# Layer 0's softmax weights from a second score product with keys on rows, and layer 1's transposes in another pair of PSUM banks

## The chip, the core and the metric

The kernel runs on one NeuronCore of one Trainium2 chip. TensorE (PE) multiplies matrices into PSUM, ScalarE (ACT) evaluates exponentials and copies, VectorE (DVE) reduces and multiplies, GpSimd (POOL) works on SBUF only, SyncE (SP) starts DMAs. Each of these engines takes its instructions in the order in which the kernel writes them. The metric is the device time of one execution in microseconds, as a median over runs.

## What is computed

Two cross-attention layers follow each other, for 8 batch elements, 256 queries of 320 channels and 20 heads of 16 channels. Cut to the core:

```python
# layer 0: 77 text keys and 179 image keys, a softmax of its own over each
out_text = attend(q, k,    v)        # attend: softmax(q k^T / 4) v
out_ip   = attend(q, k_ip, v_ip)
x1 = (out_text + out_ip) @ Wo.T + bo + x
# layer 1: 252 text keys; 4 image keys, whose scores get a term from the text weights
probs_t  = softmax(q k_t^T / 4);  text_out = probs_t @ v_t
qsem     = l2norm(probs_t @ text_ehs)
fused    = q k_ip^T / 4 + 0.5 * qsem . l2norm(ip_ehs)
ip_out   = (softmax(fused) * mask) @ v_ip
out = (text_out + ip_out) @ W_out + b_out + x1
```

All data is 32-bit floating point.

## The kernel before, in words

**Units.** Four heads of one batch element and one layer make a unit, so each layer has 5 units per element and 40 in all. The units of an element are counted g = 0 to 4. The main loop has 46 steps n (L1227): step n treats unit n of layer 0 and unit n - 6 of layer 1 (SHIFT, L47), and it finishes the values of the layer 1 unit that was begun one step earlier. Steps 0 to 39 run `both_layers` (L1148), the last six `layer_1` (L1194).

**The order is written by hand.** `tc.manual_schedule` (L79) keeps PE, DVE, ACT and POOL in the order of the source. A step is a fixed row of calls with seven gaps, numbered 0 to 6, and `fillers(n, place)` (L1023) puts work that belongs to no unit into them, from a table by g and gap: projections of queries, keys and values of both layers (`l0_q`, `l0_k`, `l0_v`, `l1_q`, `l1_k`, `l1_v`), the Gram matrix of the text (`l1_gram`), the output projections (`l0_out`, `l1_out`) and layer 1's image part.

**PSUM.** Four banks `sc0` to `sc3` hold the scores of one unit, one bank for each head (2 x 256 values on 128 partitions). Two banks `mm` serve the fillers, two banks `y` the value products.

**A unit of layer 0.** `scores` (L355) multiplies in 8 products, with queries on rows. `l0_max` (L500) takes 8 maxima on DVE. `l0_exp` (L510) runs 16 exponentials on ACT from PSUM into SBUF, one for each head, half of the queries and key group, and each sums its row. `l0_transposed` (L523) turns each head in four 128x128 transposes on PE, back into the head's own score bank, and copies the bank to SBUF (three heads on DVE, one on ACT, L407). `l0_values` (L526) multiplies by the values, with text and image kept apart in 2 x 16 rows. In the next step `l0_attn` (L545) transposes that product back to queries on rows (L553), divides by the sums on DVE (L558) and adds text and image on POOL. `l0_attn_T` (L575) transposes the whole element again for the output projection.

**A unit of layer 1.** `l1_begin` (L692) multiplies the scores into the same banks `sc0` to `sc3`. Then come 4 maxima on DVE (L716), 8 exponentials on ACT (L731), 16 transposes back into the score banks (L400) and 4 copies. In the next step `l1_values` (L742) makes, for each head and half, a product y (L755, L758) in a `y` bank and two DVE instructions that empty it (L762, L766).

**A step in old order.** Scores 0, maxima 0, exponentials 0 of heads 0 and 1, gap 0, the other exponentials; then on PE the 16 transposes of layer 0 mixed with the products y of heads 0 and 1, gaps 1 and 2, y of head 2, gap 3; scores 1, maxima 1, exponentials 1, gap 4, half of y of head 3, transposes of heads 0 and 1 of layer 1, gap 5, the other half of y, the other transposes, gap 6, values 0. Masked queries (`masked_q`, L348) come from POOL ahead of each score product.

Of the kernel before, what the change touches and what calls it, by code (L numbers as in the profile page):

```python
# [8 lines left out]
F32 = mybir.dt.float32  # L9
# [24 lines left out]
TXT0 = 77  # L34
TXT1 = 252
# [11 lines left out]
SHIFT = NQ + 1  # L47


@with_exitstack  # L50
def kernel(
# [97 lines left out]
    wo, wo1 = new_c("wo"), new_c("wo1")  # L149
# [23 lines left out]
    zeros = work.tile([P, S], F32, tag="qz", name="zeros", bufs=2)  # L173
# [5 lines left out]
    one = small.tile([P, 1], F32, tag="one", name="one", bufs=1)  # L179
    nc.vector.memset(one, 0.0)  # L180
    nc.scalar.activation(one, one, AF.Exp)
# [25 lines left out]
    for j in (5, 7):  # L207
        nc.vector.tensor_tensor(quad_m[:, 2:3], quad_m[:, 2:3], head_m[:, j : j + 1], ALU.add)

    tok_m = const.tile([P, 2], F32, tag="tok_m", name="tok_m")  # L210
    nc.gpsimd.memset(tok_m, 1.0)
    nc.gpsimd.affine_select(
        out=tok_m[:, 0:1], in_=tok_m[:, 0:1], compare_op=ALU.is_ge, fill=0.0,
        base=TXT0 - 1, pattern=[[0, 1]], channel_multiplier=-1,
    )
    nc.gpsimd.affine_select(
        out=tok_m[:, 1:2], in_=tok_m[:, 1:2], compare_op=ALU.is_ge, fill=0.0,
        base=-TXT0, pattern=[[0, 1]], channel_multiplier=1,
    )
# [29 lines left out]
    def ip_norm(_):  # L249
        nc.scalar.activation(ip["rn"], ip["rn"], AF.Sqrt)  # L250
        table(AF.Exp)
# [96 lines left out]
    def masked_q(qT, u, name):  # L348

        m, _, i = QUADS[u]  # L350
        qz = work.tile([P, S], F32, tag="qz", name=f"{name}_qz", bufs=2)
        nc.gpsimd.tensor_scalar_mul(qz, qT[:, m, :], quad_m[:, i : i + 1])  # L352
        return qz

    def scores(qz, kT, u, name):  # L355


        sc = [ps_sc.tile([P, NH, T], F32, tag=f"sc{j}", name=f"{name}_{j}") for j in range(4)]
# [12 lines left out]
    def unit(layer, b, g, sc, home):  # L371


        name = f"{layer}_{b}_{g}"
        nmx = (P, 2, NH, 2) if layer == 0 else (P, 2, NH)

        def pairs(pool, shape, tag, bufs):
            return [
                pool.tile(list(shape), F32, tag=tag, name=f"{tag}_{name}_{x}", bufs=bufs)
                for x in range(2)  # L380
            ]

        return {
            "b": b,
            "g": g,
            "sc": sc,
            "nmx": pairs(small, nmx, f"nmx{layer}", 4),
            "e": pairs(work, (P, 2, NH, T), f"e{home}", 2 + home),
            "et": pairs(work, (P, 2, 2, NH, P), f"et{home}", 2),
        }  # L390

    def transposed_probs(u, j, tn, t0, copy=None):
# [3 lines left out]
        ps = u["sc"][j][:tn].rearrange("p n t -> p (n t)")  # L396
# [16 lines left out]
    k0 = const.tile([P, NC, T], F32, tag="k0", name="k0")  # L413


    v0 = [const.tile([P, 2, H, 2, D], F32, tag=f"v0_{i}", name=f"v0_{i}") for i in range(2)]
    for t in v0:
        nc.gpsimd.memset(t[:, 1, :, 0, :], 0.0)
# [6 lines left out]
    k1c = [const.tile([P, W_K1], F32, tag=f"k1c_{i}", name=f"k1c_{i}") for i in range(2)]  # L425
# [17 lines left out]
    def l0_k(b, m):  # L443
# [19 lines left out]
        low, high, kc = slice(0, HP), slice(HP, P), k1c[b % 2]  # L463
        if m < 2:
            nc.scalar.copy(k0[:, m, first:T], ps[:, t0 + first : t0 + T])  # L465
            if kept:
                nc.gpsimd.tensor_copy(k0[:, m, :TXT0], kt[:, m, :])
        else:

            for rows in (low, high):  # L470
                nc.scalar.copy(k0[rows, m, first:T], ps[low, t0 + first : t0 + T])
                if kept:
                    nc.scalar.copy(k0[rows, m, :TXT0], kt[low, m, :])
            for rows in (low, high):
                nc.scalar.copy(kc[rows, NIP + first : T], ps[high, t0 + first : t0 + TXT1])
                if kept:
                    nc.scalar.copy(kc[rows, NIP : NIP + TXT0], kt[high, m, :])
# [3 lines left out]
    def l0_v(b, i):  # L481

        ps = mm_tile(f"v0_{b}_{i}")
        cols = slice(0, P) if i < 2 else slice(P, T)
        project_rows(ps[:, :C], lambda k: bat[b]["encT"][:, k, cols], wv if i == 0 else wvip)
        v = ps[:, :C].rearrange("p (h d) -> p h d", d=D)
        if i < 2:
            nc.scalar.mul(v0[b % 2][:, 0, :, i, :], v, tok_m[:, i : i + 1])
        else:
            nc.scalar.copy(v0[b % 2][:, 1, :, 1, :], v)  # L490

    SPAN0 = ((0, TXT0), (TXT0, T))

    def l0_begin(b, g):
        u = unit(0, b, g, scores(qz[0], lambda j: k0[:, QUADS[g][0], :], g, f"sc0_{b}_{g}"), 0)

        u["den"] = small.tile([P, NH, 4, 2], F32, tag="den0", name=f"den0_{b}_{g}")
        return u

    def l0_max(u, x):  # L500
        for j in range(2):
            for a, (t0, t1) in enumerate(SPAN0):
                nc.vector.tensor_reduce(  # L503
                    u["nmx"][x][:, j, :, a],
                    u["sc"][2 * x + j][:, :, t0:t1],
                    AX.X,
                    ALU.max,
                    negate=True,
                )

    def l0_exp(u, x):
        for j in range(2):
            for half in range(NH):
                for a, (t0, t1) in enumerate(SPAN0):
                    nc.scalar.activation(  # L515
                        u["e"][x][:, j, half, t0:t1],
                        u["sc"][2 * x + j][:, half, t0:t1],
                        AF.Exp,
                        bias=u["nmx"][x][:, j, half, a : a + 1],
                        accum_out=u["den"][:, half, 2 * x + j, a : a + 1],  # L520
                    )

    def l0_transposed(u, j, copy=None):  # L523
        transposed_probs(u, j, P, 0, copy)

    def l0_values(u):  # L526

        name = f"{u['b']}_{u['g']}"
        o = ps_y.tile([P, S], F32, tag="y", name=f"oT_{name}")
        heads = QUADS[u["g"]][1]  # L530
        for c in range(2):
            for j, h in enumerate(heads):
                nc.tensor.matmul(  # L533
                    o[j * QP : (j + 1) * QP, :],
                    v0[u["b"] % 2][:, c, h, :, :].rearrange("p a d -> p (a d)"),
                    u["et"][j // 2][:, j % 2, c, :, :].rearrange("p n s -> p (n s)"),
                    start=(c == 0),
                    stop=(c == 1),
                )
        u["rden"] = small.tile([P, NH, 4, 2], F32, tag="rden0", name=f"rden0_{name}")  # L540
        nc.vector.reciprocal(u["rden"], u["den"])
        u["o"] = work.tile([P, S], F32, tag="oT", name=f"oT_sb_{name}", bufs=1)
        nc.scalar.copy(u["o"], o)

    def l0_attn(u):  # L545
        r = bat[u["b"]]
        m, _, i = QUADS[u["g"]]
        name = f"{u['b']}_{u['g']}"
        if u["g"] == 0:
            r["attn"] = work.tile([P, NH, C], F32, tag="attn0", name=f"attn0_{name}", bufs=1)  # L550
        ps = ps_y.tile([P, S], F32, tag="y", name=f"o0_{name}")
        for half in range(NH):
            nc.tensor.transpose(  # L553
                ps[:, half * P : (half + 1) * P], u["o"][:, half * P : (half + 1) * P], ident
            )
        rden = u["rden"]
# [18 lines left out]
    def l0_attn_T(b, half):  # L575
        r = bat[b]
        r["aT", half] = attn_T(r["attn"][:, half, :], f"p0_{b}_{half}")
# [724 lines left out]
```

## Time and profile before

| | |
|---|---|
| three runs | 879.37, 879.49, 879.64 us |
| profiled execution, first to last instruction (span) | 877.6 us |
| the median stands above that span by | 1.9 us |
| PE busy | 863.8 us, 98% of the span |
| PE's weight loads busy | 696.3 us, 79% |
| DVE busy | 612.4 us, 70% |
| ACT busy | 545.0 us, 62% |
| POOL busy | 208.5 us, 24% |
| DMA | 22.96 MB, mean 26 GB/s |

The page gives no run time of the profiled execution itself beside its span; the 1.9 us lie around the span. A group row of the profile names the source line, the engine, the operation, the tiles and shapes, the number of records, then busy time and mean nanoseconds of one, then the idle time of the engine just before such instructions and what ended it. A 32-bit product of this kernel stands as two PE records, a transpose as one: 16 records are the 8 products of one unit's scores. Means of PE records overlap, so a series is priced by the time from its start to the start of what follows.

### The profile page before, as it was taken

The numbers are of one execution on the slowest core, as the hardware profiler recorded it, in microseconds if no ns is written. First come the engines' busy times: TensorE is split into PE (matmuls) and PEld (weight loads), VectorE is DVE, ScalarE is ACT, GpSimd is POOL, SyncE is SP. The second block draws the span as 40 slices with busy tenths as digits, with TensorE's granted clock in tenths as the row PEclk, the third lists the DMA queues.
The fourth block names the chain that finished last, engine by engine and source line by source line (L and its number), as shares of the span: only waits on it lengthen the run. The fifth ranks groups of instructions, "written<-read, shape, count | busy, mean of one in ns | idle before, by whom it ended". The sixth has DMA issues, their size and how long they took to land.

```text
span 877.6 us, 18756 instructions
## 1 busy us (share of the span) xinstructions
PE 863.8 (98%) x6184; PEld 696.3 (79%) x6184; DVE 612.4 (70%) x2071; ACT 545.0 (62%) x2386; POOL 208.5 (24%) x376
## 2 busy tenths in 40 slices
PE   8999999999999999999999999999999999999998
PEld 6777678788787887888877888888888788777876
DVE  2544477767776777876778678776777778875765
ACT  4774676556664686555765468654675558754855
POOL 2212311223211222122321322212222122312111
PEclk9999999999999999999999999999999999999999
DMA  9600100001000100001001010000100100000000
GB/s 279 174 6 16 44 1 1 2 18 41 15 2 20 34 25 2 15 22 43 17 1 21 16 43 1 3 20 16 43 1 1 22 16 1 1 21 1 1 20 16
DMA packets 24624, 22.96 MB, mean 26 GB/s; under 512 B 5936, under 2 KB 24496, under 8 KB 24528
## 3 DMA queue, kind: packets, MB, share of 16 engines
q1 hardware_dynamic: 23088, 20.27, 8.8%
q10 hardware_dynamic: 1440, 1.49, 0.5%
q8 instruction: 50, 0.82, 0.4%
q14 instruction: 46, 0.38, 0.1%
HBM read 18.31 MB, written 2.62 MB: 24 GB/s over the span
## 4 chain that ended last, share of the span: by engine, by line
PE 95%; ACT 3%; DVE 1%; DMA 1%; issue 0%; SPq 0%; POOL 0%; ACTq 0%; DVEq 0%
PE y L755 17%; PE sc L400 16%; PE v L325 11%; PE sc L362 10%; PE y L758 9%; PE k L313 8%; PE q L295 7%; PE p_o L338 6%; PE oT L533 5%; PE g L624 2%; ACT e L515 1%; PE p_aT_ps L331 1%; ACT e L731 1%; PE o L553 1%; PE ipo L877 1%; DMA wk<-in_WkT_dram 1%
## 5 line engine op out<-in xcount | busy, mean ns | idle before, releaser
L515 ACT ACTIVATE e<-sc,nmx 128x77 f32<-128x77 f32 (+1 forms) x640 | 227.2, 412 | 57.4 <-DVE nmx L503 57.4
L731 ACT ACTIVATE e<-sc,nmx 128x252 f32<-128x252 f32 x320 | 147.4, 484 | 120.0 <-DVE aip L711 107.3
L755 PE MATMUL y<-gv,et 126*128 126x272 f32 x640 | 202.0, 397 | 1.3
L762 DVE CUSTOM_DVE_ANT_0 e<-y,e 128x252 f32<-128x252 f32 x320 | 133.9, 419 | 90.4 <-PE y L758 81.8
L400 PE MATMUL sc<-ident,e 128*126 128x128 f32 (+1 forms) x1280 | 182.4, 274 | 4.2 <-ACT e L731 2.8
L407 DVE COPY et<-sc 128x512 f32<-128x512 f32 (+1 forms) x229 | 154.4, 689 | 24.3 <-PE sc L400 14.5
L503 DVE TENSOR_REDUCE nmx<-sc 128x2 f32<-128x154 f32 x320 | 109.7, 416 | 87.2 <-PE sc L362 87.2
L400 PEld LDWEIGHTS sc<-ident,e 128*126 128x126 f32 (+1 forms) x1280 | 149.1, 140 | 14.2 <-ACT e L731 6.2
L515 ACT ACTIVATION_READ_ACCUMULATOR e<-sc,nmx 128x1 f32 x640 | 159.9, 250 | 0.0
L758 PEld LDWEIGHTS y<-gv,et 126*128 126x128 f32 x640 | 120.7, 189 | 25.9
L758 PE MATMUL y<-gv,et 126*128 126x146 f32 x640 | 131.4, 287 | 0.0
L716 DVE TENSOR_REDUCE nmx<-sc 128x2 f32<-128x504 f32 x160 | 106.7, 673 | 22.7 <-PE sc L362 22.7
L755 PEld LDWEIGHTS y<-gv,et 126*128 126x128 f32 x640 | 104.8, 190 | 18.2 <-issue 3.0
L568 POOL TENSOR_TENSOR attn<-o_sb 128x64 f32<-128x64 f32 x80 | 24.0, 321 | 396.3 <-DVE o_sb L558 355.2
L407 ACT COPY et<-sc 126x512 f32<-126x512 f32 (+1 forms) x91 | 52.2, 593 | 75.8 <-PE sc L400 75.7
L362 PE MATMUL sc<-k,sc_qz 32*128 32x256 f32 x1152 | 82.6, 400 | 1.0 <-ACT k L465 0.6
L352 POOL TENSOR_SCALAR sc_qz<-q,quad_m 128x256 f32<-128x256 f32 x80 | 73.2, 925 | 6.6 <-ACT q L302 6.0
L362 PEld LDWEIGHTS sc<-k,sc_qz 32*128 32x128 f32 x1152 | 52.1, 184 | 24.4 <-issue 15.3
L731 ACT ACTIVATION_READ_ACCUMULATOR e<-sc,nmx 128x1 f32 x320 | 69.7, 218 | 0.0
L325 PE MATMUL v<-wv,encT 128*126 128x324 f32 (+1 forms) x192 | 58.1, 447 | 0.0
L766 DVE COPY num<-y 128x20 f32<-128x20 f32 x320 | 55.6, 174 | 0.0
L338 PE MATMUL p_o<-wo,p_aT 128*128 128x320 f32 x180 | 53.0, 437 | 0.3 <-DVE p_aT L332 0.3
(148 smaller groups left out, 1044.7 us busy)
## 6 DMA issues: line engine op xcount, KB each, us to landing
encT<-in_encT_dram SPq DMA_DIRECT2D x7, 512.0 KB
x<-in_x_dram SPq DMA_DIRECT2D x8, 320.0 KB
out_dram<-osb SPq DMA_DIRECT2D x15, 160.0 KB
xT<-in_xT_dram SPq DMA_DIRECT2D x7, 256.0 KB
texts<-in_encT_dram SPq DMA_DIRECT2D x6, 154.0 KB
xT<-in_xT_dram SPq DMA_DIRECT2D x7, 128.0 KB
vip_rows<-vipA SPq DMA_DIRECT2D x32, 25.0 KB
wv<-in_WvT_dram SPq DMA_DIRECT2D x1, 640.0 KB
```

The source lines that it names most:

```text
L325: nc.tensor.matmul(ps, lhsT(k), w[:, k, :], start=(k == 0), stop=(k == NE - 1))
L338: nc.tensor.matmul(ps[:, :C], aT[:, m, :], w[:, m, :], start=(m == 0), stop=(m == NC - 1))
L362: nc.tensor.matmul(sc[j][:, half, :], qz[rows, half * P : (half + 1) * P], kT(j)[rows, :], start=True, stop=True,)
L400: nc.tensor.transpose(v[:, c, half, :], u["e"][x][:, i, half, t0 + c * tn : t0 + (c + 1) * tn], ident,)
L407: copy(u["et"][x][:tn, i].rearrange("p c n s -> p (c n s)"), ps)
L503: nc.vector.tensor_reduce(u["nmx"][x][:, j, :, a], u["sc"][2 * x + j][:, :, t0:t1], AX.X, ALU.max, negate=True,)
L515: nc.scalar.activation(u["e"][x][:, j, half, t0:t1], u["sc"][2 * x + j][:, half, t0:t1], AF.Exp, bias=u["nmx"][x][:, j, half, a : a + 1], ...
L716: nc.vector.tensor_reduce(u["nmx"][x][:, j, :], u["sc"][2 * x + j][:, :, t0 : t0 + TXT1], AX.X, ALU.max, negate=True,)
L731: nc.scalar.activation(u["e"][x][:, j, half, t0 : t0 + TXT1], u["sc"][2 * x + j][:, half, t0 : t0 + TXT1], AF.Exp, bias=u["nmx"][x][:, j, ...
L755: nc.tensor.matmul(y, et[:, 1 - odd, half, :], gv[0][:, g, full], start=True, stop=False)
L758: nc.tensor.matmul(y[:, into], et[:, odd, half, :], gv[1][:, g, part], start=False, stop=True)
L762: nc.vector.tensor_tensor_reduce(e, y[:, g0 : g0 + TXT1], e, op0=ALU.mult, op1=ALU.add, scale=1.0, scalar=0.0, accum_out=r["n2"][:, half, ...
```

## The change

Layer 0's scores with queries on rows are still made, and their maxima and exponentials, but the exponentials now write back in place in PSUM and only their sums are wanted. The logarithm of the sum is taken on ACT (`l0_log`), and minus maximum minus logarithm is written by DVE into two columns of each head's 32 in a zeroed tile (`l0_shift`). Two PE transposes turn that tile, and DVE adds it to the masked queries (`l0_shifted_q`), in rows where the mask had left zeros. The keys `kq` carry ones in those rows, one row for text keys and one for image keys. A second score product with keys on rows (`l0_probs`) then gives shifted scores, and four exponentials of 128x512 give weights that are already normalised and already turned. The value product of all units of 128 channels adds up in one bank, text and image together, with channels on rows as the output projection wants them (`aT0`).

So these go: 16 transposes of weights and 4 copies in each layer 0 unit, the back transposes, the division, the POOL additions, and `l0_attn_T`. The keys of layer 0 are masked and offset by head group when they are copied from PSUM (`own`, on DVE and POOL). Layer 1's transposes go to the `y` banks in place of the score banks, which `l0_probs` uses next. The row of calls in a step and the table of fillers are rewritten. The activation tables are set by name to a set with both exponential and logarithm. `WoT`'s last 64 rows are loaded twice.

```diff
-    def l0_exp(u, x):
-        for j in range(2):
+    def l0_sums(u, x):
+
+        for j in (2 * x, 2 * x + 1):
             for half in range(NH):
                 for a, (t0, t1) in enumerate(SPAN0):
                     nc.scalar.activation(
-                        u["e"][x][:, j, half, t0:t1],
-                        u["sc"][2 * x + j][:, half, t0:t1],
+                        u["sc"][j][:, half, t0:t1],
+                        u["sc"][j][:, half, t0:t1],
                         AF.Exp,
...
+    def l0_log(u):
+        nc.scalar.activation(u["den"], u["den"], AF.Ln)
+    def l0_shift(u):
+        t = shift[QUADS[u["g"]][2]].rearrange("p n (j x) -> p n j x", j=4)
+        spans = ((0, 4, (D, 0)[u["g"] % 2]),) if u["g"] < 4 else ((0, 2, D), (2, 4, 0))
+        for j0, j1, at in spans:
+            nc.vector.tensor_tensor(
+                t[:, :, j0:j1, at : at + 2], u["nmx"][:, :, j0:j1, :], u["den"][:, :, j0:j1, :],
+                ALU.subtract,
+            )
+    def l0_shifted_q(u):
+        t = shift[QUADS[u["g"]][2]]
+        ps = mm_tile(f"shift_{u['b']}_{u['g']}")
+        for half in range(NH):
+            nc.tensor.transpose(ps[:, half * P : (half + 1) * P], t[:, half, :], ident)
+        nc.vector.tensor_tensor(u["qz"], ps[:, :S], u["qz"], ALU.add)
+    def l0_probs(u):
+        name = f"0_{u['b']}_{u['g']}"
+        sc = score_banks(f"p{name}")
+        for c in range(2):
+            for j in range(4):
+                rows = slice(j * QP, (j + 1) * QP)
+                nc.tensor.matmul(
+                    sc[j][:, c, :],
+                    kq[rows, u["g"], c * P : (c + 1) * P],
+                    u["qz"][rows, :],
+                    start=True,
+                    stop=True,
+                )
+        u["et"] = keys_first(0, name)
+        for j in range(4):
+            nc.scalar.activation(
+                u["et"][j // 2][:, j % 2].rearrange("p c n s -> p (c n s)"),
+                sc[j].rearrange("p c s -> p (c s)"),
+                AF.Exp,
+            )
...
-    def both_layers(n, u, v1):
+    def both_layers(n, us, v1):
+        u0 = l0_begin(b, g)
+        qz[1] = queries(1, n)
         for pair in range(2):
             l0_max(u0, pair)
+        l0_sums(u0, 0)
         fillers(n, 0)
+        l0_sums(u0, 1)
+        l0_log(u0)
+        part(l1_values, v1, 0)
         fillers(n, 1)
+        part(l1_values, v1, 1)
+        part(l1_values, v1, 2)
         fillers(n, 2)
+        part(l1_values, v1, 3)
+        l0_shift(u0)
+        fillers(n, 3)
+        l0_shifted_q(u0)
+        qz[0] = queries(0, n + 1)
         u1 = begin1(n)
         for pair in range(2):
             part(l1_max, u1, pair)
         part(l1_exp, u1, 0)
         fillers(n, 4)
         part(l1_exp, u1, 1)
+        for j in range(4):
+            if u1:
+                ps = ps_y.tile([P, NH * S], F32, tag="y", name=f"eT_{n}_{j}")
+                l1_transposed(u1, j, ps=ps)
+            if j == 1:
+                fillers(n, 5)
+        l0_probs(u0)
         fillers(n, 6)
+        us = us + [u0]
+        if g in (1, 3, 4):
+            l0_values(us)
+            us = []
```

The new table of fillers for a full element (gap: work; `now`, `last`, `old`, `ahead` are the element and its neighbours):

```python
(0, 0): [(l0_out, last, 0), (l0_out, last, 1)],
(0, 1): [(l0_q, now, (2,)), (l1_image, old)],
(0, 3): [(l1_xT, last)],
(0, 4): [(l1_k, last, 0)],
(0, 6): [(l1_q, last, (0, 1))],
(1, 0): [(l0_k, now, 1)],
(1, 2): [(l1_q, last, (2,))],
(1, 4): [(l1_k, last, 1)],
(1, 6): [(l0_v, now, 1)],
(2, 0): [(l1_ip, now), (l1_v, now, 0)],
(2, 1): [(l1_den, old), (l1_norm, old)],
(2, 4): [(l0_k, now, 2), (l1_fused, old)],
(2, 6): [(l1_gram, now, 0), (l1_fused_exp, old)],
(3, 0): [(l1_v, now, 1)],
(3, 2): [(l1_probs, old)],
(3, 4): [(l0_q, ahead, (0, 1))],
(3, 5): [(l1_probs_T, old), (l1_text, old)],
(3, 6): [(l1_gram, now, 1), (l0_k, ahead, 0)],
(4, 0): [(l1_attn, old)],
(4, 2): [(l1_attn_T, old, 0), (l1_attn_T, old, 1)],
(4, 4): [(l0_v, ahead, 0)],
(4, 5): [(l1_out, old, 0)],
(4, 6): [(l1_out, old, 1)],
```

## The prediction

> **What bounds the kernel now.** I first read the busy shares, then the chain that ended last. A steady element comes from the busy times by stretch: five steps, 398.5 to 502 us.
>
> ```profile
> PE 863.8 (98%) x6184; PEld 696.3 (79%) x6184; DVE 612.4 (70%) x2071; ACT 545.0 (62%) x2386; POOL 208.5 (24%) x376
> PE 95%; ACT 3%; DVE 1%; DMA 1%; issue 0%; SPq 0%; POOL 0%; ACTq 0%; DVEq 0%
> sum 103.50, PE 103.45 PEld 85.18 DVE 77.74 ACT 65.00 POOL 25.41; mean PE 20.69 PEld 17.04 DVE 15.55 ACT 13.00 POOL 5.08
> ```
>
> TensorE (PE) sets the end: in a steady element it stands still for 0.05 us of 103.5. ScalarE (ACT) has 38 us of slack in that element. So PE work that goes is gained only if PE stays as full as it is. Where the cover comes from is seen in the chain of waits, from layer 1's scores of a step on:
>
> ```profile
> 409.77 1.07 PE sc L362 x16
> 410.85 1.90 PE k L313 x8
> 412.75 0.46 PE y L755 x2
> 413.21 0.25 PE y L758 x2
> 413.46 0.89 PE sc L400 x8
> 414.35 1.70 PE g L624 x8
> 416.05 0.46 PE y L755 x2
> 416.51 0.25 PE y L758 x2
> 416.76 0.88 PE sc L400 x8
> 417.63 1.00 PE oT L533 x16
> ```
>
> While ACT makes layer 1's exponentials, PE works on a filler, a product y, a filler, another y. Step 6 has no y yet, and the timeline shows what then happens:
>
> ```profile
> 101.24 1.97 PE L624 MATMUL g<-encT 128*126 128x252 f32 x8
> 103.24 0.65 PE L400 MATMUL sc<-ident,e 128*126 128x128 f32 x4
> 104.14 0.66 PE L400 MATMUL sc<-ident,e 128*126 128x128 f32 x4 [0.25 <-ACT e L731]
> 105.55 0.66 PE L400 MATMUL sc<-ident,e 128*126 128x128 f32 x4 [0.75 <-ACT e L731]
> 106.45 0.66 PE L400 MATMUL sc<-ident,e 128*126 128x128 f32 x4 [0.25 <-ACT e L731]
> 107.04 1.07 PE L533 MATMUL oT<-et,v 128*32 128x256 f32 x16
> ```
>
> From the end of the scores (101.24) to the last transpose (107.04) are 5.8 us, of which PE has 1.80 + 4 x 0.44 = 3.6 us of work: 2.2 us are lost. That is the order the change gives every step: all y stand ahead of layer 1's scores, so I price by this stretch.
>
> **PE work.** The chain gives 0.44 us for 4 transposes, 1.07 for a unit's scores, 0.22 for 2 transposes (L553), 0.71 for a y. A layer 0 unit loses 16 transposes (1.75) and 2 back (0.22), and gains the second scores (1.07, same shapes as L362) and 2 shift transposes (0.22): -0.68. An element loses 6 transposes of `l0_attn_T` (0.66). Per element 5 x -0.68 - 0.66 = -4.1 us; in all -32.5. Values 0 keep their 1.0 us a unit, `l0_v` its 24 records.
>
> **ACT and DVE work.** ACT gains four 512-wide exponentials: nearest rows L407 and L302, 512 wide, 0.59 to 0.60 each, some 0.5 in series. It gains a logarithm of 16 columns (0.24 by the square root L798) and loses a 512 copy in most units (0.59). That makes about 15 us of a 20 us step, no bound. DVE loses three 0.69 copies and the division (0.42) a unit, gains an addition (0.42 by L558), a subtraction (0.16 to 0.24 by L208 and L541) and key copies (0.2 to 0.33, between L558 and shorter ones). In-place exponentials have no row; I keep L515's pace, 16 in 5.5 us, and bound them by 0.5 us a unit either way, since their output port changes. POOL's extra masks and SP's one more weight load stand far ahead of their use: nothing.
>
> **Stall 1, layer 1's exponentials.** In the steady stretch the first starts 0.87 after the scores, eight follow at 0.45 and copies of the filler between them add 0.4, so the last transpose ends 5.6 after the scores (5.8 in step 6). PE has 1.76 of transposes plus gaps 4 and 5.
> - g = 0 and 1: `l1_k`, 1.9. Lost 5.6 - 3.7 = 1.9 each.
> - g = 2: `l0_k` of 1.2 or 2.4, with 6 to 9 small ACT copies (0.25 to 0.37, some 1.2 in series) ahead of the second half of the exponentials. Lost 6.5 - 3.6 = 2.9.
> - g = 3: `l0_q` 2.6 and 0.2. Lost 1.0.
> - g = 4: `l0_v` 4.4 and `l1_out` 1.6 cover it.
>
> Sum 7.7 us an element; bounds half of it (exponentials earlier than in step 6) and all.
>
> **Stall 2, the shift's round trip.** `l0_shift` waits on DVE behind the two instructions that empty the last y, and PE's next instruction is the shift transpose; behind it on PE queue scores 1 and all that hang on them. From y's end: L762 and L766 took 0.56 (409.77 to 410.33 in the timeline), a subtraction 0.17, the hand-over to PE some 0.07: 0.8 us. For g = 0 the gap 3 filler `l1_xT` hides it, but the shift waits for a buffer that its copy (L332, 0.55) empties, some 0.3. Sum 4 x 0.8 + 0.3 = 3.5 us; a whole one stays as long as the y are in this place. The logarithm itself ends 0.87 + 5.5 + copies + 0.24 = 6.7 to 8.0 after scores 0, and PE has 5.7 us of y and 1.7 to 5.2 us of fillers until there: covered. If a first-half exponential should wait for all 8 maxima (new layout of one tile), it ends 1.2 later and g = 2 and 3 pay some 0.5.
>
> **Stall 3, y behind DVE's queue.** Maxima 0 hold DVE for 2.74 us after scores 0. With two y banks, the third y waits until DVE has emptied the first. The 16 transposes that stood between the y gave DVE time. g = 4: gap 0 is `l1_attn`, 1.1 of PE, and its two DVE additions (0.48) stand first too, so the third y starts at 4.25 in place of 2.5: 1.75. g = 1: 0.6 to 1.3 behind the key copies. g = 2 and 3: 0.6 and 0.3 behind reciprocals and sums of layer 1. Some 3.8 us in all; since the trace shows no such run of y here, bounds nothing and 3.8, and I take half, 1.9.
>
> **Stall 4, the end of a step.** The banks come free 2.2 us after the second scores (a 512 copy, then four exponentials). Gap 6 and the values cover it but for g = 2 (1.7 of `l1_gram`: 0.5) and g = 4 (0.2): 0.7; bounds 0 and 0.7.
>
> **The first steps.** Steps 0 to 6 began at 11.4, 22.9, 33.7, 44.7, 58.8, 70.8 and 89.9, step 7 at 108.0. A unit of layer 0 alone now has the serial path 0.87 + 5.5 + 0.24 + 0.2 + 0.22 + 0.42 + 1.07 + 2.2 + 1.07 = 11.8, with hand-overs 12.3, against steps of 10.8 to 12.0. With values at g = 1 (1.0 more) and `l0_v` of 4.4 now in step 2: +1.4, +3.2, +5.3, +0.9, +2.5, -3.5 (step 5 has less), +1.7, which is +11.5; I take +10, bounds 0 and 15.
>
> **Sum.** Per element 7.7 + 3.5 + 1.9 + 0.7 - 4.1 = 9.7 us. Steps 7 to 39 are 6.6 elements: 64 us. With the first steps 877.6 + 64 + 10 = 951.6 us span; the last six steps keep their order. The page gives only the span; the median lies 1.9 above it, so **953.5 us**.
>
> **Two rules of the Trainium skill.** The granted clock is 1.00 in every stretch, also in the first 100 us, where PE stood still for 4.5 us in pieces. "TensorE: Matmul & The Clock Gate", in its first part, says that idle windows of about 3.4 us halve the clock; by it, my stalls of at most 2.9 us leave it alone, and with it halved all PE times above would double where it holds. The profile has 21 table loads of 1283 ns. "ScalarE: Activation LUTs", section on table sets, says that exponential and logarithm share a set and need no reload between them; by it the logarithms load nothing, and otherwise each would cost a switch to and fro, 2.6 us of loads by the row.
>
> **Rivals.**
> 1. *PE stays full.* ACT has slack, so its exponentials might be ready in time. With stalls 1, 3 and 4 gone, 3.5 - 4.1 = -0.6 an element, 6.6 x -0.6 = -4, first steps 0: 875.5 us; with stall 2 gone too 879.5 - 32.5 = 847. It decides from stalls under 4.1 us an element. For it: PE's 0.05 us of idle time now. Against it: step 6's 2.2 us with a filler as long as that of g = 0 and 1. Chance 0.07, at 875.5.
> 2. *Only half.* Stall 1 at half, 3 and 4 nothing, first steps nothing: 3.85 + 3.5 - 4.1 = 3.25, times 6.6 = 21: 900 us; to about 930 with one of them. For it: in step 6 no old y waits for DVE. Chance 0.23.
> 3. *The change doesn't do what it says:* the named set isn't kept and each logarithm reloads tables. 80 loads of 1.28 us on ACT, half of them ahead of the shift; some 0 to 1.3 us a step: 980 to 1000. For it: the page shows loads at each change of function (L798, L789). Chance 0.05.
> 4. *No change* within 0.2%: stalls just at 4.1. Chance 0.02.
>
> The forecast, 930 to 985, has the remaining 0.63. Range: low end rival 2's 900; high end with stall 3 whole 6.6 x 11.6 = 77, first steps 15, maxima waits 10: 877.6 + 102 + 1.9 = 981.5, taken as 985. About 0.2% (1.8 us) is what a measurement here can tell from no change. Faster by more 0.07, within 0.02, slower by more 0.91.
>
> **What would show it.** PE's busy time falls to about 835 us while the span grows to 950; group rows of L400's layer 1 transposes show tens of us of idle time released by ACT's exponentials (stall 1: 50); the shift transposes have idle time released by DVE (25 to 30); the y products have some released by DVE's emptying (10 to 25). ACT's busy time rises to some 630. Wrong would be: those three rows near zero, or table loads far above 21.

## The result, and the profile after

The changed kernel takes 1063.8 us (median of 4 runs, 1061.3 to 1067.5) against 879.5: ratio 1.210, 95% interval 1.207 to 1.213. The direction was forecast, the size was not: 953.5 us, with a range from 900 to 985. The profiled execution has a span of 1060.2 us, 182.6 more than before.

The page of the changed kernel, in the order of before: busy shares, the clock in 40 slices, the chain that ended last.

```profile
PE 932.2 (88%) x6144; PEld 678.6 (64%) x6144; DVE 546.6 (52%) x1992; ACT 655.4 (62%) x2508; POOL 197.2 (19%) x310
PEclk9788998999999998899999999899999999999999
PE 68%; ACT 18%; DVE 9%; issue 4%; DMA 1%; POOL 0%; SPq 0%; DVEq 0%; ACTq 0%
```

PE is no longer the whole chain: ACT has 18% of it and DVE 9%. PE's busy time rose by 68 us although it has less to do, and the clock, 1.00 everywhere before, falls below 0.9 in seven slices of the page. In all, 82 us of the span are at half clock (the expectations below say 83 or 84, with a stretch that begins as the span ends).

Four of its group rows (busy and mean, then the idle time before them and what ended it):

```profile
L539 ACT ACTIVATE sc<-sc,nmx 128x77 f32<-128x77 f32 (+1 forms) x640 | 218.3, 341 | 70.4 <-DVE nmx L530 52.7
L794 PE MATMUL y<-gv,et 126*128 126x272 f32 x640 | 207.2, 405 | 25.1 <-DVE num L805 17.2
L401 PE MATMUL eT<-ident,e 128*126 128x128 f32 x544 | 100.6, 302 | 28.7 <-ACT e L770 18.5
L565 PE MATMUL shift<-ident,shift 128*128 128x128 f32 x80 | 18.3, 313 | 53.0 <-DVE shift L555 45.6
```

PE stands 53.0 us ahead of the shift transposes, 28.7 ahead of layer 1's transposes and 25.1 ahead of y; these three rows hold 107 of the 123 us for which PE's records leave gaps (before: 9). Step 7 begins at 145.1 us in place of 108.0 (+37.1); steps 7 to 38, from the start of step 7 to the start of step 39, take 801.4 in place of 660.0 (+141.4); the rest takes 4.1 more. These are 32 steps or 6.4 elements, where the prediction reckoned with 6.6.

The stretch that answers to the steady element of before, steps 20 to 24 (470.8 to 595.8 us), in the busy times by stretch:

```profile
sum 124.99, PE 111.88 PEld 81.84 DVE 69.20 ACT 79.37 POOL 23.84; mean PE 111.88 PEld 81.84 DVE 69.20 ACT 79.37 POOL 23.84
```

These are 13 us of PE's pauses, where there were 0.05. One g = 2 in PE's timeline, from the shift transposes on:

```profile
401.52 0.44 PE L565 MATMUL shift<-ident,shift 128*128 128x128 f32 x2 [0.80 <-DVE shift L555]
401.89 1.15 PE L372 MATMUL sc<-k,sc_qz 32*128 32x256 f32 x16
402.96 1.48 PE L319 MATMUL k<-encT,wkip 128*128 128x179 f32 x8
404.52 1.91 PE L401 MATMUL eT<-ident,e 128*126 128x128 f32 x8
408.50 2.26 PE L401 MATMUL eT<-ident,e 128*126 128x128 f32 x8 [2.07 <-ACT e L770]
```

The 0.80 is the forecast round trip. The 2.07 is stall 1: no y is left between the filler (402.96) and the transposes, and the last exponentials are late, since ACT has the filler's key copies (405.83 to 407.86) ahead of them.

I added up PE's records by function, each counted from the end of the one before. The span's +182.6 is +114.2 of idle time and +68.4 of busy time:

| part | us |
|---|---|
| idle ahead of shift transposes | +53 |
| idle ahead of layer 1's transposes (28.7 against 4.2) | +24 |
| idle ahead of y (25.1 against 1.3) | +24 |
| other idle time | +13 |
| work removed, as the prediction has it | -32 |
| 74.9 us of PE work at half clock, half of it | +37 |
| 640 transposes at 0.157 in place of 0.115 each (full clock) | +27 |
| y's 1280 records, 250.7 in place of 233.8 | +17 |
| shift transposes at 0.215 each in place of 0.11 | +8 |
| scores and the rest, not separated | +11 |

So waits are most of the loss (114 of 182.6 us), and the records of transposes and y are longer too. That they are longer because PE's work no longer overlaps is a reading of this table, not shown by an experiment.

### The profile page after: what moved, and what is told of

It reads as the page before. It is cut to its first block, busy times and chain, and to the rows that moved or that the text cites. A ratio compares the mean times of both kernels' runs of the same rounds, so it can differ in the third digit from the quotient of the medians.

```text
span 1060.2 us, 18478 instructions
## 1 busy us (share of the span) xinstructions
PE 932.2 (88%) x6144; PEld 678.6 (64%) x6144; DVE 546.6 (52%) x1992; ACT 655.4 (62%) x2508; POOL 197.2 (19%) x310
## 4 chain that ended last, share of the span: by engine, by line
PE 68%; ACT 18%; DVE 9%; issue 4%; DMA 1%; POOL 0%; SPq 0%; DVEq 0%; ACTq 0%
PE y L794 12%; PE sc L372 9%; PE v L331 8%; ACT e L770 8%; ACT sc L539 7%; PE q L301 6%; PE y L797 6%; PE p L575 5%; PE oT L600 5%; PE p_o L344 5%; PE eT L401 3%; DVE nmx L530 3%; PE k L319 2%; PE g L658 2%; PE shift L565 2%
## 5 line engine op out<-in xcount | busy, mean ns | idle before, releaser
L539 ACT ACTIVATE sc<-sc,nmx 128x77 f32<-128x77 f32 (+1 forms) x640 | 218.3, 341 | 70.4 <-DVE nmx L530 52.7
L794 PE MATMUL y<-gv,et 126*128 126x272 f32 x640 | 207.2, 405 | 25.1 <-DVE num L805 17.2
L401 PE MATMUL eT<-ident,e 128*126 128x128 f32 x544 | 100.6, 302 | 28.7 <-ACT e L770 18.5
L539 ACT ACTIVATION_READ_ACCUMULATOR sc<-sc,nmx 128x1 f32 x640 | 124.8, 195 | 0.0
L401 PEld LDWEIGHTS eT<-ident,e 128*126 128x126 f32 x544 | 64.5, 146 | 65.7 <-ACT e L770 55.3
L584 ACT ACTIVATE et<-p 128x512 f32<-128x512 f32 x160 | 82.6, 602 | 33.9 <-PE p L575 33.9
L408 DVE COPY et<-eT 126x512 f32<-126x512 f32 x102 | 68.4, 685 | 48.4 <-PE eT L401 46.8
L671 POOL COPY gv<-gv 126x1134 f32<-126x1134 f32 (+1 forms) x17 | 34.3, 2019 | 169.8 <-ACT gv L667 169.8
L770 ACT ACTIVATION_READ_ACCUMULATOR e<-sc,nmx 128x1 f32 x296 | 63.3, 214 | 0.0
L372 PE MATMUL sc<-kq,sc_qz 32*128 32x256 f32 x640 | 52.3, 408 | 3.2 <-ACT et L584 2.3
L575 PE MATMUL p<-sc_qz,kq 32*128 32x256 f32 x640 | 51.7, 440 | 2.3 <-DVE sc_qz L566 2.3
```

The source lines that it names most:

```text
L372: nc.tensor.matmul(sc[j][:, half, :], qz[rows, half * P : (half + 1) * P], kT(j)[rows, :], start=True, stop=True,)
L401: nc.tensor.transpose(v[:, c, half, :], u["e"][x][:, i, half, t0 + c * tn : t0 + (c + 1) * tn], ident,)
L539: nc.scalar.activation(u["sc"][j][:, half, t0:t1], u["sc"][j][:, half, t0:t1], AF.Exp, bias=u["nmx"][:, half, j, a : a + 1], accum_out=u[" ...
L575: nc.tensor.matmul(sc[j][:, c, :], kq[rows, u["g"], c * P : (c + 1) * P], u["qz"][rows, :], start=True, stop=True,)
L584: nc.scalar.activation(u["et"][j // 2][:, j % 2].rearrange("p c n s -> p (c n s)"), sc[j].rearrange("p c s -> p (c s)"), AF.Exp,)
L770: nc.scalar.activation(u["e"][x][:, j, half, t0 : t0 + TXT1], u["sc"][2 * x + j][:, half, t0 : t0 + TXT1], AF.Exp, bias=u["nmx"][x][:, j, ...
```

## The experiments

All edits are to the changed kernel, except for three that start from the kernel before. "First steps" is the start of step 7 in the profiled execution, 145.1 us in the changed kernel.

### The sums' exponentials

Theory: the sums are slow because they write in place. The changed kernel's timeline of ACT, and then that of the kernel before (start, duration):

```profile
473.30 0.38 ACT L539 ACTIVATE sc<-sc,nmx 128x179 f32<-128x179 f32 x1
473.60 0.19 ACT L539 ACTIVATION_READ_ACCUMULATOR sc<-sc,nmx 128x1 f32 x1
473.83 0.30 ACT L539 ACTIVATE sc<-sc,nmx 128x77 f32<-128x77 f32 x1
...
474.58 0.19 ACT L539 ACTIVATION_READ_ACCUMULATOR sc<-sc,nmx 128x1 f32 x1
474.68 0.29 ACT L539 ACTIVATE sc<-sc,nmx 128x77 f32<-128x77 f32 x1
```

```profile
400.99 0.40 ACT L515 ACTIVATE e<-sc,nmx 128x179 f32<-128x179 f32 x1
401.29 0.20 ACT L515 ACTIVATION_READ_ACCUMULATOR e<-sc,nmx 128x1 f32 x1
401.38 0.32 ACT L515 ACTIVATE e<-sc,nmx 128x77 f32<-128x77 f32 x1
```

Before, the next exponential starts 0.39 us after the 179-wide one, while the sum is still being read out (401.38 is ahead of 401.29 + 0.20). In place it starts after 0.53 us, when the reading out is over; only where the bank changes (474.58 to 474.68) does it start early again. The 16 of a unit take 7.7 us in place of 6.2 (medians over the 40 units).

Sums into SBUF:

> One edit to the changed kernel: the 16 exponentials that only serve the sums of layer 0 write to a tile in SBUF instead of back over the scores in PSUM. Theory A (in place, each exponential waits for the one before it in the same bank, so that the logarithm comes 1.6 to 1.9 us later a unit and the shift with it): the 16 exponentials of a steady unit fall from 7.4 us to 5.5 to 5.8 us; the shift transposes' wait of 2.5 us at g = 3 falls to some 0.8; the seven first steps give back 7 x 1.7 = 12 us, the 32 later ones about 1.7 us an element, 11 us: 1064 - 23 = 1041 us. If the halved clock (about 83 us of the span in all) follows from these waits, up to 37 us more go: 1004 us at the least, and the mean clock rises from 0.96 towards 1. Rival B (the exponentials are slow for another reason, or late scores are covered): 7.4 us stays, or the time moves by less than 5 us.

```diff
-  u["sc"][j][:, half, t0:t1],          # output
+  e[:, j % 2, half, t0:t1],            # tile of u["et"], allocated earlier
   u["sc"][j][:, half, t0:t1],
```

Still in place, but neighbours in two banks:

> One edit to the changed kernel: the exponentials stay in place in PSUM, but two neighbours never hit the same bank (the loop over the two banks becomes the innermost). It tells two reasons for the slow sums apart. Theory A1 (each waits for its neighbour's write to the same bank to be over): the neighbour is now in another bank, the 16 fall from 7.4 us to 5.5 to 6 us as when they write to SBUF, and the time falls as much as there, to about 1041 us or less. Rival A2 (writing to PSUM is slower in itself): 7.4 us stays and the time stays at 1060 us and above.

```diff
-        for j in (2 * x, 2 * x + 1):
-            for half in range(NH):
-                for a, (t0, t1) in enumerate(SPAN0):
+        for half in range(NH):
+            for a, (t0, t1) in enumerate(SPAN0):
+                for j in (2 * x, 2 * x + 1):
```

Measured 1035.5 and 1042.4 us; the 16 take 6.2 us in both. In the profiled executions the first steps give back 9 us each and steps 7 to 38 give 13 and 11. Theory A1 holds as far as it says that an exponential waits for its neighbour in the same bank. The traces show what it waits for: in the changed kernel 480 of the 640 exponentials (all but the first in each bank) carry a wait for a semaphore of ACT itself, which the reading out of the exponential before raises, and they start 0.03 us after it. With SBUF none carries one. With two banks in turn most still do, but 543 start ahead of the end of their neighbour's reading out (97 in the changed kernel). So the program orders neighbours in one tile, which here is one bank; that the bank itself would make them wait is not shown. The write to PSUM itself is not slow: with two banks in turn a record is 376 ns, in SBUF 407 ns.

```profile
L539 ACT ACTIVATE sc<-sc,nmx 128x179 f32<-128x179 f32 (+1 forms) x640 | 222.3, 376 | 63.0 <-DVE nmx L530 60.8 <-PE sc L372 2.2
```

```profile
L544 ACT ACTIVATE et<-sc,nmx 128x77 f32<-128x77 f32 (+1 forms) x640 | 225.6, 407 | 55.0 <-DVE nmx L530 50.8 <-PE sc L372 4.2
```

The first row is of the kernel with two banks in turn, the second of that with SBUF. The Trainium skill, "ScalarE: Activation LUTs", section "Step-by-step: what each stage is for", says that an activation into PSUM is faster than one into SBUF. The single record agrees (341 ns in the changed kernel and 376 with two banks in turn, against 407 into SBUF). The pace of a pair does not (0.97 and 0.77 us against 0.69), and the pace counts.

### The shift transposes behind layer 1's scores

> One edit to the changed kernel: the two shift transposes go behind layer 1's scores, and their addition on DVE behind layer 1's first maxima, so that PE has 1.07 us of scores while the shift makes its round trip over DVE. Theory (stall 2: PE stands 53 us in all ahead of the shift transposes, some 15 of them in the first seven steps, which have no layer 1 scores and stay as they are): waits of 0.8 us go, waits of 2.5 us fall to about 1.4: 30 us less, 1034 us; up to 15 us more if the clock is then halved less often, 1019 us. Rival (the addition now holds up layer 1's second maxima and exponentials, and the wait only moves on to layer 1's transposes): idle time ahead of those grows from 29 us to over 45 and the time falls by less than 10 us.

```diff
-        l0_shifted_q(u0)
         qz[0] = queries(0, n + 1)
         u1 = begin1(n)
-        for pair in range(2):
-            part(l1_max, u1, pair)
+        ps = l0_shift_T(u0)                 # the two transposes
+        part(l1_max, u1, 0)
+        l0_shifted_q(u0, ps)                # the addition
+        part(l1_max, u1, 1)
```

Measured 1030.2 us, 33.6 less. The row of the shift transposes, 53.0 us of idle time before, has 12.0 left, nearly all in the first steps:

```profile
L565 PE MATMUL shift<-ident,shift 128*128 128x128 f32 x80 | 18.5, 315 | 12.0 <-DVE shift L555 11.4
```

Steps 7 to 38 gain 31.0; idle time ahead of layer 1's transposes there grows by 3 and ahead of scores by 7. Stall 2 was there, with the late logarithm on top of it. The timeline of the changed kernel at g = 3 shows both:

```profile
553.40 0.41 PE L797 MATMUL y<-gv,et 126*128 126x146 f32 x2
556.34 0.44 PE L565 MATMUL shift<-ident,shift 128*128 128x128 f32 x2 [2.53 <-DVE shift L555]
```

2.5 us, where the prediction had 0.8 and a logarithm that is "covered".

### Four banks for y

> One edit to the changed kernel: the two PSUM banks for projections and the two for the products y become one ring of four. Theory E (with two banks a y waits until DVE has read the y two before it; a run of y takes 0.88 us each in place of 0.71): the y of a run go at 0.71, 0.17 x 6 to 8 = 1.0 to 1.3 us a step, 33 to 43 us in 33 steps: 1021 to 1031 us. Rival (the time is then lost at the shift, which waits for the logarithm or for DVE, since y's are only a stretch ahead of it): the y's go at 0.71, the shift transposes wait longer by the same amount, and the time falls by less than 10 us.

```diff
-    ps_mm = ... tile_pool(name="ps_mm", bufs=2, space=PS)
-    ps_y = ... tile_pool(name="ps_y", bufs=2, space=PS)
+    ps_y = ... tile_pool(name="ps_y", bufs=4, space=PS)    # all [P, 512] tiles
```

Measured 1042.3 us, 21.5 less, between theory (33 to 43) and rival (under 10). In a run of y, from the second on, one follows the other after 0.71 us in place of 0.97 (medians; the theory had 0.88 for the latter), and y's PE records fall from 250.7 to 236.2 us. But their idle time stays (23.8): y now waits for the fillers' copies on ACT, which share the ring (16.0 us for `gv` alone). The waits ahead of layer 1's transposes stay too (28.4 against 28.7). Waits of PE, 340 to 600 us, in that kernel:

```profile
PE shift L564 <- DVE shift L554: 10.7, 10, 1.8
PE y L793 <- ACT gv L684: 5.1, 4, 1.8
PE eT L400 <- ACT e L769: 5.0, 6, 2.1
PE y L793 <- ACT q L307: 1.8, 3, 0.6
```

### The clock

> Products whose result nobody reads (128x128 by 128x256, some 0.43 us each by the Gram products' rows) are added to the changed kernel where PE stands still: 6 ahead of the shift transposes in the first seven steps (12 in step 2) and at g = 3, 2 in the other steps, 4 between layer 1's transposes at g = 2. Nothing else is changed, and no wait is taken away. Theory (the clock is halved in the 84 us that follow PE's waits of about 2 us and more; the PE work of those 84 us takes 38 us longer by it): the stretches at half clock fall from 84 us to under 15, the mean granted clock rises from 0.96 to 0.99 and more, and the time falls by some 30 us in spite of 0 to 5 us that the added products run over the waits: 1034 us. Rival (the half clock follows something else than PE's pauses): 70 us and more at half clock, 1060 us and above.

```diff
+    def keep_busy(n, times):
+        ps = mm_tile(f"busy_{n}")
+        for i in range(times):
+            nc.tensor.matmul(ps[:, :S], ident, wv[:, 0, :S], start=True, stop=True)
...
+        keep_busy(n, 12 if n == 2 else 6 if n < SHIFT + 1 or g == 3 else 2)
         l0_shifted_q(u0)
```

Half clock fell from 82 to 14 us, the mean clock rose to 0.994, and the time stayed: 1063.2 us. The added products ran 80 us and took the place of only some 50 us of idle time, so this kernel doesn't price the clock. With products where the long waits are, and no more than fit:

> As the kernel that was kept busy (there the stretches at half clock fell from 84 to 14 us, but its added products ran 80 us and stood in for only 52 us of pauses, so that the time stayed), with products only where PE stands still for about 2 us and more and no more than fit: 5, 5 and 12 ahead of the shift transposes of steps 0, 1 and 2, 5 at g = 3 from step 8 on, 4 between layer 1's transposes at g = 2. Theory (half clock costs what the PE work in it loses, 38 us for 84 us): some 25 us at half clock are left in the first steps, the others go: 1064 - 27 + 2 = 1039 us. Rival (PE's longer pace at half clock only fills waits that would stand there anyway, for ACT and DVE set the end of those stretches): the half clock goes, but the time falls by less than 10 us, to 1054 us and above.

Measured 1047.8 us, 16 less, between theory and rival: 51 us of half clock went (82 to 31), which is 0.31 us of time for each, what the added products cost themselves included. So the whole of PE's longer pace doesn't show in the time; the rival's reason, that some of it fills waits for ACT and DVE, fits but was not tested. At that price all 82 us are worth an estimated 25 us. The clock row of this kernel:

```profile
PEclk9898999999999999999999999999999999999999
```

### The last head's y, and a tile that the change took away

> One part of the change undone: the two products y of the last head of a unit go back between layer 1's transposes (one ahead of the first four, one ahead of the third four); the other six stay ahead of layer 1's scores. Theory D (stall 1 of the prediction: the cover that the y gave layer 1's exponentials is gone): 1.4 us of PE work return to that window, g = 0, 1 and 2 lose 1.4 us less each and g = 3 up to 1.0 less: 5 us an element, 33 us in 6.6 elements. But the same 1.4 us are then missing ahead of the shift, and where the logarithm is late (g = 2, g = 3 and the first steps) they come back as a longer wait of the shift transposes: 1064 - 33 + 2 x 6.6 x 1.4 = 1049 us, between 1031 and 1064. Rival (the late y have no part in the loss): no change, or a loss of over 5 us from the later logarithm alone.

```diff
-        part(l1_values, v1, 3)
         l0_shift(u0)
...
         for j in range(4):
+            if j % 2 == 0:
+                part(l1_values, v1, 3, (j // 2,))
```

Measured 1147.7 us: 84 worse where 15 better was expected. I blamed the ring of two banks that y and transposes share. So the transposes went back to the score banks, with the same late y:

> The second part of the change undone: layer 1's transposes go back into its own score banks, and the two y of the last head back between them, as in the kernel before. Theory (the y in layer 1's window cover its exponentials, if the transposes don't take the same two banks from them): the transposes' idle time falls from 29 us to below 15 and no wait of y on the transposes' copies is added, some 25 us gained; against it the second scores of layer 0 must wait for the last copy out of a score bank, 0.8 to 1.0 us a step, 27 to 33 us, and the logarithm loses 1.4 us of cover at g = 2 and g = 3 and in no first step, 15 us: 1064 - 25 + 30 + 15 = 1084 us, bounds 1060 and 1110, and far below the 1148 us of the kernel that moved the y alone. Rival 1 (moving the transposes was the main loss): 1030 us or less. Rival 2 (the loss with late y comes from the later logarithm alone): 1140 us or more again.

1177.3 us: that theory fell, and rival 2 too, for the idle time ahead of the transposes rose from 26 to 62 us in steps 7 to 38 beside that ahead of the shift (40 to 60). Nor did the other three edits mend it:

> Four edits together: the sums' exponentials write to SBUF (28 us gained alone), one ring of four banks for projections and y (21 gained alone), the shift transposes behind layer 1's scores, and the last head's y between layer 1's transposes (which alone lost 84 us, by a ring of two banks that y and transposes shared and by a later logarithm, both mended here). Theory (each edit takes a wait of its own): 1064 - 28 - 21 - 30 - 20 = 965 us, between 940 and 1000, with the mean clock above 0.98. Rival (the waits stand in for each other, what one edit frees the next wait takes): 1010 us and above. The kernel before, 879 us, would be beaten only if less than 4 us of waits an element and nothing in the first steps were left, which neither theory expects.

1028.5 us. The same three edits without late y:

> Three of the edits together: the sums' exponentials into SBUF (28 us alone), one ring of four banks (21 alone), shift transposes behind layer 1's scores (34 alone); the last head's y stay ahead of layer 1's scores. Theory (the three waits are apart but for the late logarithm at g = 3, some 10 us that the first and the third edit both mend): 1064 - 28 - 21 - 34 + 10 = 991 us, between 975 and 1005; then the late y were what held the kernel with four edits at 1028 us. Rival (the waits stand in for each other): 1010 us and above, as with four edits.

962.5 us, better than the theory's 991. So the late y itself costs 66 us there. The timelines of DVE and ACT in the kernel with four edits name the reason:

```profile
484.03 0.08 DVE L807 DVE_READ_ACCUMULATOR2_ANT n<- 128x1 f32 x1
```

```profile
484.15 0.47 ACT L776 ACTIVATE e<-sc,nmx 128x252 f32<-128x252 f32 x1 [1.88 <-DVE n L807]
```

Layer 1's fifth exponential waits until DVE has read the old weights e in the last y's product. The diff has it in one line that I had passed over: before, `e` of layer 1 had `2 + home` = 3 tiles (`home` is 1 while both layers run), now it has 2, so the second exponentials write where the late y still reads.

```diff
-            "e": pairs(work, (P, 2, NH, T), f"e{home}", 2 + home),
...
+            "e": pairs(work, (P, 2, NH, T), f"e{home}" if home else "et0", name, 2 if home else 4),
```

That was tried in the kernel before:

> The kernel before, with 2 tiles e in place of 3 for layer 1 and nothing else changed. Theory: the four second exponentials of a layer 1 unit must wait until DVE has read the old e in the last late y's product, which stands on PE behind the first eight transposes; after that come 1.8 us of exponentials before the next transpose can run, some 2 us of wait a step, 33 times: 66 us, 945 us, between 920 and 980 with what the clock adds. Rival (the third tile was never needed): below 885 us.

```diff
-            "e": pairs(work, (P, 2, NH, T), f"e{home}", 2 + home),
+            "e": pairs(work, (P, 2, NH, T), f"e{home}", 2),
```

980.0 us (ratio 1.115, 1.113 to 1.117), at the upper end of the forecast: one tile fewer costs the kernel before 101 us (45 us of the span are then at half clock). Its waits (total, times, longest); in the kernel before, the second row is absent and PE's wait is 2.8 us:

```profile
ACT e L731 <- DVE aip L711: 107.8, 34, 6.6
ACT e L731 <- DVE n L762: 97.1, 33, 4.5
PEld sc L400 <- ACT e L731: 83.2, 73, 2.2
PE sc L400 <- ACT e L731: 66.3, 72, 1.9
```

So with two tiles the y can't stay late. The changed kernel with three tiles was not run. What their earlier place costs, with layer 1's transposes in the y banks, was measured in the kernel before:

> The second part of the change alone, made in the kernel before: layer 1's transposes go to the y banks, and the last head's two y stand ahead of layer 1's scores; layer 0 keeps its old weights, with transposes between the other y. Theory (stall 1: the exponentials of layer 1 lose the cover of 2 x 0.71 us of y, and those 1.4 us stay as a wait at g = 0 to 3): PE has 0.05 us of idle time an element before, so 5.7 to 7.7 us an element come, 38 to 51 us in 6.6 elements, and up to 10 us from the clock at g = 2: 925 us, between 905 and 945. Rival (the wait ahead of layer 1's transposes in the changed kernel comes from its fuller ACT, with the sums and the second exponentials, and not from the place of the y): below 890 us.

```diff
+        part(l1_values, v1, 3)              # ahead of layer 1's scores
...
+        for j in range(4):
+            if u1:
+                ps = ps_y.tile([P, NH * S], F32, tag="y", name=f"eT_{n}_{j}")
+                l1_transposed(u1, j, ps=ps)
```

923.8 us, 44.7 more, as the theory has it: 43 of them in steps 7 to 38, none in the first steps. And with the transposes moved, the y left late:

> The kernel before, with layer 1's transposes in the y banks and nothing else changed: the last head's two y stay between them, and e keeps its 3 tiles. Theory (the tile e, not the banks, makes late y dear): the y and the transposes wait for the copies out of two banks for up to 0.3 us at two places in a step at the most, below 20 us in all: 879 to 900 us, well below the 924 us of the kernel that moved the y ahead too. Rival (the shared ring of two banks is what costs): 924 us and above.

914.2 us, 34.9 more, between theory and rival. The two banks cost 35 us even with the y in their old place: PE's idle time grows by 20 us and its records by 14. Of the idle time ahead of the transposes 9.5 us wait for DVE to empty a y and 8.0 for the exponentials. Moving the y as well adds 10; what the shared banks cost with the y ahead was not measured apart.

### What is left

> The three edits, with products whose result nobody reads where PE still stands still for long: 3, 3 and 7 in steps 0, 1 and 2, 4 between layer 1's transposes at g = 2. Theory: the stretches at half clock of the three edits (estimate 50 us) fall below 25 us and the time falls by some 10 us more, to 980 us. Rival (half clock costs little, because other engines set the end there): no more than 3 us. Under either theory the kernel before, 879 us, stays ahead, since the waits ahead of layer 1's transposes (some 50 us with their longer pace) and the first steps (some 20 us) are left.

949.5 us, 13.1 less than the three edits alone for 41 us of half clock (48 to 7), 0.32 for each, close to the price above. By the spans of the profiled executions in place of the medians the two prices are 0.29 and 0.37, so some 0.3 is as much as can be said. It is the fastest version, and 8% slower than before (ratio 1.079, 1.077 to 1.082).

> The kernel with three edits (963 us), and the last head's two y on PE directly behind layer 1's scores and the shift transposes, ahead of the filler; DVE empties them between layer 1's first and second maxima, so that their old e is read before the second exponentials want its tile. Theory (late y only hurt where they hold e): 1.4 us of PE work fill the window of layer 1's exponentials, 5 us an element less: 963 - 30 = 933 us, between 920 and 950. Rival (the second maxima come 1.2 us later behind DVE's emptying and the exponentials with them): no gain, 960 us and above.

> The same, with products whose result nobody reads in steps 0, 1 and 2 alone (3, 3 and 7). With the three edits, such products gained 13 us, of which 5 to 6 in the first steps and 9 at g = 2, where this kernel has y in place of them. Theory: 6 us less than without them, 927 us. The kernel before (879 us) stays ahead under both theories: the first steps alone stand 12 us behind it and y's waits of 11 us are left.

959.2 and 956.2 us: 3 and 6 us less than 962.5, where 30 and 36 were forecast; the rival holds in the total. The second maxima do come later, 2.8 us behind the first in place of 1.7 (medians), since DVE empties the y between them; single steps (g = 0: 22.1 against 23.1 us) gain and others lose. What decides in those others stays open. In the fastest version, step 7 starts at 120.6 us (12.6 late) and steps 7 to 38 take 715.2 (55 more than before); PE stands 16.8 us ahead of layer 1's transposes there and 11.5 ahead of y. For comparison, in these steps the second part alone cost the kernel before 43 us, and the work removed is worth 26 by the prediction's sum.

## Why the prediction was wrong

The mechanism was right: work leaves PE, and PE loses more by standing still than it gains. What failed are sizes: stall 2, by a logarithm that was called covered; stall 3, by the pace of y; the clock, put at nothing; and the first steps. The forecast is short by 110 us: 27 in the first steps, 79 in steps 7 to 38 and 4 behind them. For steps 7 to 38, with the forecast taken for their 6.4 elements:

| term | forecast, us | measured, us |
|---|---|---|
| stall 1 | 49 | 50: idle time 24, longer transposes 25 |
| stall 2 | 22 | 47: idle time 40, longer shift transposes 7 |
| stall 3 | 12 | 38: idle time 22, longer y 16 |
| stall 4 | 4.5 | 1 |
| work removed | -26 | not measured apart |
| half clock | nothing | 20: half of 39 us of PE work |
| not separated | | 11, with the work as forecast |
| sum | 62 | 141 |

- **Stall 1, right in its sum.** The second part alone cost 44.7 us in the kernel before. The split was not foreseen: half of it is longer transposes, and the idle time is 2.0 us a step at g = 2, where 2.9 was forecast, and only 0.7 at g = 0 and 1, where 1.9 was. The shared banks had no price in the forecast; alone they cost the kernel before 35 us.
- **Stall 2, right as a wait, wrong in size.** The round trip of 0.8 us was right: the trace has 0.80 at g = 1 and 2 and 0.96 at g = 4. At g = 3 it has 2.5, at g = 0 1.17 where 0.3 was forecast (the wait for the copy of `l1_xT`), and 12 us more stand in the first steps. The step that failed is the logarithm: "In-place exponentials have no row; I keep L515's pace ... and bound them by 0.5 us a unit either way". They took 1.5 us longer a unit (7.7 against 6.2), and "covered" was false at g = 3 and in the first steps. With the sums in SBUF the wait at g = 3 falls to 1.0 and 28.3 us of time are gained. The note on the output port looked at the wrong thing: what cost time was the wait for the exponential before.
- **Stall 3, bounded right and chosen wrong.** The hand sum had 3.8 an element and I took half. Waits for y in steps 7 to 38 are 22.6 us, 3.5 an element, and a further 16 come from y's pace: 0.97 us each from the second of a run on, where I used 0.71 from a place with transposes between. Four banks brought 0.71 back.
- **Stall 4, wrong and small:** 0.7 an element forecast, 0.8 us of idle time ahead of scores in all of steps 7 to 38.
- **The first steps: +10 forecast, +37.1 measured.** Idle time is 21 of the 37, and the rest is about half of the 33 us of PE work that ran at half clock there. The in-place sums were 9 us; with the three edits 19.5 are gone, with the products against the half clock 24.5, and 12.6 are left, near the 10 forecast. With the sums alone at the old pace 27.9 are left, half clock on 24 us of PE work among them; so it is not shown that the serial path was right for the old pace.
- **The clock: nothing forecast, 82 us at half clock,** worth an estimated 25 us. Waits of up to 2.9 us were to leave it alone; see below.
- **Rivals.** None came. No added table loads (rival 3): 21, as before. PE's busy time rose to 932 where 835 was forecast; 37 us of that are half clock, the others are the longer records of the table above. ACT's came to 655 (630 forecast).

The separate stalls also feed each other: three edits worth 28, 21 and 34 us alone gave 101 together. One part of these 18 us can be estimated: half clock fell from 82 to 48 us with them, as with no one of them (61, 89, 78), which at 0.31 is 5 us more than the three alone; the others stay open.

## What to carry to other kernels

Ahead of pricing a change by its engine work, list every ring of tiles whose depth the diff alters and every place where two users now share a ring: one tile less cost the kernel before 101 us, more than any single edit gained. A pace measured between other work is no price for the same instruction in a run, and the pace of an instruction that writes elsewhere is no price for one that writes over its own input, where the program may order neighbours. PE, at 98% before, lost with its cover also part of its clock: half clock came with its pauses.

## What the runs showed of the hardware

- Activations with a sum (77 and 179 wide), in series in place in one PSUM bank, each with a wait for the one before: 0.97 us a pair, against 0.69 into SBUF and 0.77 in place with two banks in turn.
- Half clock comes in stretches of 3.4 us or multiples, and within a trace all 233 starts lie on one grid of 3.41 us. In the 17 traces after the change and of the experiments, 81 of 99 PE pauses of 1.9 us and more had such a stretch begin close to them (from 1 us before to 3 us after), as had 118 of 567 pauses of 0.7 to 1.6 us. "TensorE: Matmul & The Clock Gate" of the Trainium skill, Part 1, tells of a free-running window of that length, which fits the stretches. But the prediction read it as needing a pause of the whole window; here a pause of 2 us mostly did. Shorter ones add up: cut into the windows of that grid, at full clock, PE's idle time in a window below 1.2 us was followed by half clock in 28 of 4268 cases, 1.2 to 1.8 us in 89 of 272, and 1.8 us or more in 110 of 120.
- Half clock cost some 0.3 us of time per us in two pairs of kernels, the added products included; half the clock with PE always the bound would be 0.5.
